# A four-layer transformer step on one core: queries moved ahead, layer norm and routing of the last batch in smaller steps, expert gathers six ahead

## The chip, the cores and the metric

The kernel runs on 1 core of a Trainium2 chip. The metric is device microseconds of one launch; the median of three runs is given. The engines in what follows: TensorE (PE) multiplies matrices, VectorE (DVE) and ScalarE (ACT) work on tiles of 128 rows, GpSimd (POOL) does the same more slowly and issues the indirect DMAs, SyncE (SP) issues most plain DMAs.

## What is computed

Four batches of 512 rows of 256 numbers, all in float32. Four layers, each added to x:

```
x = x + xattn0(layernorm(x), ctx)     # 1 head, 1601 context rows
x = x + ffn0(layernorm(x))            # 8 heads, 8 experts a head, hard gate, causal attention
x = x + xattn1(layernorm(x), ctx)     # 16 heads, masked, output projection
x = x + moe(layernorm(x))             # 32 experts, the best 8 a row, capacity 256

def moe(x):                           # x: 2048 x 256
    probs = softmax(x @ gate.T)       # 2048 x 32
    topw, topi = top_k(probs, 8);  topw /= topw.sum(-1)
    flat_e = topi.reshape(-1)
    pos = place of each choice in its expert's list, in order of the rows
    buf[flat_e, pos] = x[row]         # 32 x 256 x 256; places from 256 on are dropped
    h = silu(buf @ gate_half.T) * (buf @ up_half.T)      # 192 wide
    eo = h @ down.T
    return sum over the 8 choices of topw * eo[flat_e, pos]
```

## The kernel before

The 2048 rows of x are 16 tiles of 128 rows (NT = 16), four to a batch (TB = 4), and stay on the chip through all layers. A scheduler orders the first attention and the routing's own instructions by the order in the program; the second attention and the experts are ordered by hand, as generators whose steps are run between bursts of TensorE work: a `yield` is a place where the other stream gets its turn.

*First attention* (lines 180 to 312). `fold_weights` multiplies the query and key weights into one (TensorE `pw`, `pb`). `queries(b)` takes a batch's layer norm, transposes it (`tp_xn`, line 153), multiplies it by the folded weight (`pq`, line 225) and by the folded bias (`pc`, line 237). The loop over 16 tiles then makes scores (`sc`, line 255), their maximum on VectorE, the exponentials `pr` on ScalarE (line 267), and, one tile behind, transposes of the probabilities (`tp`, line 394), the sum over context rows (`po`, line 403) and, two tiles behind, the projection (`tp_o`, line 415; `pf`, line 421). The queries of batch b + 1 are made in two pieces, at tiles 2 and 3 of batch b. The loads stand on SyncE's queue: x of batch 0, weights, context of batch 0 transposed and by rows, value weight, then x of the other batches.

*Second attention* (lines 1178 to 1472). A burst of TensorE work makes scores for one stretch of keys (`sa`, line 1171, for the maxima `mx` on VectorE, line 1174; `sb`, line 1458, for the exponentials on ScalarE, line 1463, into probability tiles `pt`) and the sums `pv` (line 1391). Between bursts, steps of the next batch's projection and of the last batch's routing run. `finish(b)` (line 1355) closes a batch: it projects (`pf`, line 1372), adds to x (line 1375), two tiles a step, then hands over to `route_steps`.

*Layer norm*. `variances` (line 117) takes statistics of the four tiles (lines 122 and 123). `moments` takes the root by ScalarE's Sqrt (line 131) and a reciprocal; `moments_root` (line 95) takes it by a starting guess and three rounds of Newton's rule on small tiles (lines 101 to 113), on GpSimd, or on VectorE for the last batch.

*Routing* (`route_steps`, line 1647). For a batch: layer norm, transposes (line 1665), logits (1673), softmax, top-8 of each row (1700, 1701), a running count that gives each choice its place, weights (1737). Then for each tile one-hots: `r_lb` (VectorE, line 1742) of the place modulo 8, `r_hold` of it times the row's number (ScalarE, 1748) and times its weight (GpSimd, 1749), `r_ha` of the place over 8 (VectorE, 1753). 32 small products (`ph`, line 1761) put numbers and weights at their places; line 1766 adds them to `held`. Each of `r_lb`, `r_hold` and `r_ha` has one buffer. `slots` (line 1771) spreads `held` out into lists of rows (`ids`) and weights. Routing of batches 0 to 2 runs between bursts of the next batch's attention; that of the last batch has nothing beside it.

*Experts* (`experts1`, line 1475). For each of 32 experts: load weights (four ahead), gather its 256 rows by two indirect DMAs on GpSimd (line 1498), AHEAD = 8 experts ahead, transpose (line 1508), up-projection (`gu`, `gr`, line 1521), down-projection (`po_e`, line 1537), scaling on ScalarE (`eo`, line 1543), and an addition to the output rows by two indirect DMAs on GpSimd (line 1549). Additions of one expert wait until those of the expert before have landed, as they can add to the same rows. GpSimd issues gathers and additions in program order. The order at the heart:

```python
                for e in range(E1):
                    if e + 4 < E1:
                        load(e + 4)
                    if e + AHEAD < E1:
                        gather(e + AHEAD)
                    if e + 1 < E1:
                        transpose(e + 1)
                    up(e)
                    if e:
                        down(e - 1)
```

Of the kernel before, what the change touches and what calls it, by code (L numbers as in the profile page):

```python
# [12 lines left out]
F32 = mybir.dt.float32  # L13
# [3 lines left out]
ALU = mybir.AluOpType  # L17
# [4 lines left out]
P = 128  # L22
B, S, D = 4, 512, 256
S2 = 1601
NT = B * S // P
TB = S // P
# [13 lines left out]
Q1 = 401  # L40
LO = 8
HI = CAP // LO
AHEAD = 8
NO_SLOT = 4096.0

NEG = -3.0e38
# [6 lines left out]
class Program:  # L53
# [38 lines left out]

        return self.normed(b, pool, *self.moments(b, pool))

    def moments_root(self, b, pool, eng):


        nc = self.nc
        mv = self.variances(b, pool)
        v = pool.tile([P, TB], F32, name="ln_v")  # L100
        nc.vector.tensor_scalar(v, mv[:, :, 1], EPS, None, ALU.add)
        i = pool.tile([P, TB], I32, name="ln_i")
        nc.vector.tensor_scalar(i, v.bitcast(I32), 1, None, ALU.arith_shift_right)
        nc.vector.tensor_scalar(i, i, -1.0, float(0x5F3759DF), ALU.mult, ALU.add)
        h = pool.tile([P, TB], F32, name="ln_h")
        nc.vector.tensor_scalar(h, v, -0.5, None, ALU.mult)  # L106
        rstd = pool.tile([P, TB], F32, name="ln_rstd")
        y, a = i.bitcast(F32), v
        for _ in range(4):
            eng.tensor_tensor(a, y, y, ALU.mult)  # L110
            eng.tensor_tensor(a, a, h, ALU.mult)
            eng.tensor_scalar(a, a, 1.5, None, ALU.add)
            eng.tensor_tensor(rstd, a, y, ALU.mult)
            y = rstd
        return mv, y

    def variances(self, b, pool):
        nc = self.nc
        mv = pool.tile([P, TB, 2], F32, name="ln_mv")
        for t in range(TB):  # L120
            st = pool.tile([P, 6], F32, name="ln_st")
            nc.vector.bn_stats(st, self.xs[b * TB + t])
            nc.vector.bn_aggr(mv[:, t, :], st)
        return mv

    def moments(self, b, pool):

        nc = self.nc
        mv = self.variances(b, pool)
        rstd = pool.tile([P, TB], F32, name="ln_rstd")  # L130
        nc.scalar.activation(rstd, mv[:, :, 1], AF.Sqrt, bias=self.eps)
        return mv, rstd
# [54 lines left out]
    def xattn0(self, ve, oe, outer, dram):  # L187
# [3 lines left out]
        with ExitStack() as es:  # L191
# [13 lines left out]
            bk = self.load_column(wp, "L0_bk")  # L205
            ctxT, ctx, q = {}, {}, {}
            ctxT[0] = self.load_chunks(0, big)
            ctx[0] = self.load_rows(0, rows)
            wv = self.load_split(wp2, "L0_Wv", D)
            bv = self.load_row(wp2, "L0_bv")  # L210
            self.load_x(range(TB, NT))
            wg = self.f0_wg = self.load_split(outer, "F0_wg", H0 * E0)
            self.f0_xnT, self.f0_gate = {}, {}
            wqk, qb = self.fold_weights(wq, wk, bq, wp, ps_m)
            self.mask_scan(self.cp, scan, dram)

            def queries(b):

                xnT = self.transposed(self.layernorm(b, p1), p1, ps_m, "mm")
# [23 lines left out]
                q[b] = qT, kb  # L243
                yield

            for _ in queries(0):
                pass
            pending, late = None, None
            for i in range(NT):
                b, t = divmod(i, TB)  # L250
# [35 lines left out]
                            self.d[w][:, :P].rearrange("(k p) f -> p k f", p=P),  # L286
                        )
                project = self.xattn0_project(*late, wv, p2, ps_m) if late is not None else None
                if t == TB - 1 and b + 1 < B:
                    next(queried)  # L290
                late = None
                if pending is not None:
                    late = self.xattn0_sum(
                        *pending, ctx[(i - 1) // TB], bv, p2, ps_m, ps_o, project
                    )
                if t == TB - 2 and b + 1 < B:
                    queried = queries(b + 1)
                    next(queried)
                if t == 0 and b:
# [878 lines left out]
    def xattn1_keys(self, router):  # L1178
# [9 lines left out]
        with ExitStack() as es:  # L1188
# [41 lines left out]
            def project(b):  # L1230

                ctxT = ctx[b] = self.load_context(b, p1)
                mv, rstd = self.moments_root(b, p1, nc.gpsimd)
                yield True
                xn = self.normed(b, p1, mv, rstd, root=False)
                add_bias(b)
# [117 lines left out]

            def finish(b):

                for t0 in range(0, TB, 2):
                    oTs = []
                    for t in (t0, t0 + 1):
# [8 lines left out]
                    for t, oT in zip((t0, t0 + 1), oTs):  # L1368
                        x = self.xs[b * TB + t]
                        pf = ps_s.tile([P, D], F32, tag="s", name="pf")  # L1370
                        for k in range(2):
                            nc.tensor.matmul(  # L1372
                                pf, oT[:, k, :], fo[:, k, :], start=(k == 0), stop=(k == 1)
                            )
                        nc.vector.tensor_tensor(x, pf, x, ALU.add)
                    yield
                yield from router.route_steps(b, p1, ps_s, "s", ps_s, "s")

            def run(steps):
                for _ in steps:  # L1380
# [94 lines left out]
    def experts1(self, router):  # L1475
# [3 lines left out]
        with ExitStack() as es:  # L1479
# [85 lines left out]
            with tc.manual_schedule():  # L1565
# [5 lines left out]
                for e in range(E1):  # L1571
                    if e + 4 < E1:
                        load(e + 4)
                    if e + AHEAD < E1:
                        gather(e + AHEAD)
                    if e + 1 < E1:
                        transpose(e + 1)
                    up(e)
                    if e:
                        down(e - 1)  # L1580
                down(E1 - 1)

# [1 line left out]
class Router:  # L1584
# [59 lines left out]
        for _ in self.route_steps(b, p1, ps1, "s", pst, "t"):  # L1644
            pass

    def route_steps(self, b, p1, ps1, tag1, pst, tagt):

        nc, prog = self.nc, self.prog
        sh = [P, TB, E1]  # L1650
        last = b == B - 1
        mv, rstd = prog.moments_root(b, p1, nc.vector if last else nc.gpsimd)
        yield True
        xn = prog.normed(b, p1, mv, rstd, root=False)
        for t in range(b * TB, (b + 1) * TB):
            nc.sync.dma_start(prog.out[t * P : (t + 1) * P, :], prog.xs[t])
        nc.sync.dma_start(
# [38 lines left out]

        top = p1.tile([P, TB, TOPK], F32, name="r_top")
        rest = p1.tile(sh, F32, name="r_rest")
        for t in range(TB):
            nc.vector.max(top[:, t, :], pr[:, t, :])  # L1700
            nc.vector.match_replace(rest[:, t, :], top[:, t, :], pr[:, t, :], -1.0)
# [34 lines left out]
        nc.vector.reciprocal(den, den)  # L1736
        nc.vector.tensor_tensor(pr, pr, wide(den), ALU.mult)
        yield
        for t in range(TB):
            ll = [P, E1, LO]  # L1740
            lb = p1.tile(ll, F32, name="r_lb")
            nc.vector.tensor_tensor(  # L1742
                lb, lo[:, t, :].unsqueeze(2).to_broadcast(ll),
                self.count[:, :LO].unsqueeze(1).to_broadcast(ll), ALU.is_equal,
            )
            hold = p1.tile([P, E1, 2, LO], F32, name="r_hold")
            i = b * TB + t
            nc.scalar.activation(hold[:, :, 0, :], lb, AF.Copy, scale=self.tok1[:, i : i + 1])
            nc.gpsimd.tensor_tensor(  # L1749
                hold[:, :, 1, :], lb, pr[:, t, :].unsqueeze(2).to_broadcast(ll), ALU.mult  # L1750
            )
            ha = p1.tile([P, E1, HI], F32, name="r_ha")
            nc.vector.tensor_tensor(
                ha, hi[:, t, :].unsqueeze(2).to_broadcast([P, E1, HI]),
                self.count.unsqueeze(1).to_broadcast([P, E1, HI]), ALU.is_equal,
            )
            yield True
            ph = ps1.tile([P, E1 // 4, 2 * LO], F32, tag=tag1, name="ph")
            for g in range(E1 // 4):
                for s in range(4):  # L1760
                    nc.tensor.matmul(
                        ph[32 * s : 32 * s + 32, g, :], ha[:, 4 * g + s, :],
                        hold[:, 4 * g + s].rearrange("p v l -> p (v l)"), start=True, stop=True,
                        tile_position=(0, 32 * s),
                    )
            nc.vector.tensor_tensor(self.held, ph, self.held, ALU.add)
            yield
        if b == B - 1:
            self.slots(p1, ps1, tag1)

    def slots(self, p1, ps1, tag1):

# [115 lines left out]
```

## Time and profile before

| | us |
|---|---|
| three runs | 2241.95, 2233.48, 2243.65 |
| their median | 2241.95 |
| the profiled execution | 2232.17, its span 2230.3 |
| granted TensorE clock, mean of the span | 0.966 |
| last batch's routing, last `pf` to first gather | 1936.7 to 1981.35 |
| experts, first gather to the end | 1981.35 to 2230.3 |

In the profile's lines, times are microseconds from the start of the span. A line of the timeline has the start, the duration, the engine, the line of the kernel, the operation, output<-inputs, the shapes, and in brackets the idle time of the engine before it with what ended it. `PEclk` gives the clock that TensorE was granted in each of 40 slices, in tenths.

### The profile page before, as it was taken

How to read it: one execution, taken by the hardware profiler on the slowest of the kernel's cores; microseconds unless marked ns; L12 is line 12 of the kernel's file. 1: busy time of each engine (PE TensorE's matmuls, PEld its weight loads, DVE VectorE, ACT ScalarE, POOL GpSimd, SP SyncE). 2: the span in 40 equal slices, each digit the busy share in tenths (PEclk: the TensorE clock that was granted, in tenths of full speed). 3: DMA queues.
4: the chain of work that ended last, by engine and by line, in shares of the span. 5: the costliest groups of instructions: out<-in, count | busy, mean ns of one | idle time of the engine just before them, and what ended most of it. 6: DMA issues, size and time to landing. Idle time of an engine off the chain costs nothing.

```text
span 2230.3 us, 29813 instructions
## 1 busy us (share of the span) xinstructions
PE 2063.4 (93%) x11446; PEld 1066.8 (48%) x11446; DVE 1191.7 (53%) x1953; ACT 715.3 (32%) x1523; POOL 806.9 (36%) x865
## 2 busy tenths in 40 slices
PE   6999999999999999988999999999999999859893
PEld 4667754444444544334444444444444444347561
DVE  5344345445555444565657757785678775232220
ACT  1222221112122121103545545554455555412121
POOL 9999444545444444422100100010001000047764
PEclk9999999999999999999999999999999999969986
DMA  6473121122122223224221222123121200037763
GB/s 211 134 254 104 52 70 56 50 57 57 41 61 74 63 68 62 52 54 100 60 47 29 67 57 38 38 59 66 21 49 31 45 16 2 19 118 178 168 142 38
DMA packets 98190, 161.89 MB, mean 73 GB/s; under 512 B 20100, under 2 KB 68760, under 8 KB 97528
## 3 DMA queue, kind: packets, MB, share of 16 engines
q1 hardware_dynamic: 79800, 126.00, 22.2%
q0 software_dynamic: 17664, 33.38, 7.4%
q8 instruction: 93, 1.52, 0.3%
q14 instruction: 57, 0.47, 0.1%
q10 hardware_dynamic: 576, 0.52, 0.1%
HBM read 137.28 MB, written 22.31 MB: 72 GB/s over the span
## 4 chain that ended last, share of the span: by engine, by line
PE 50%; DVE 7%; DMA 4%; issue 2%; POOL 1%; ACT 1%; POOLq 0%; SPq 0%; ACTq 0%; DVEq 0%
PE sb L1458 12%; PE sa L1171 10%; PE pv L1391 8%; DVE mx L1174 4%; DMA out<-eo,ids 3%; PE acc L589 3%; PE py L885 2%; PE pv L1281 2%; PE po_e L1537 2%; PE pk L1253 2%; PE gu L1521 2%; POOL out L1549 1%; PE pf L1372 1%; DMA qd<-kc 1%; PE gr L1521 1%
## 5 line engine op out<-in xcount | busy, mean ns | idle before, releaser
L1174 DVE TENSOR_REDUCE mx<-sa 128x2 f32<-128x802 f32 x512 | 495.1, 990 | 139.1 <-PE sb L1458 72.4
L1463 ACT ACTIVATE pt<-sb 128x512 f32<-128x512 f32 (+1 forms) x832 | 429.6, 604 | 309.9 <-PE sb L1458 287.4
L1171 PE MATMUL sa<-kq,qq 32*128 32x401 f32 x2048 | 467.6, 542 | 35.6 <-DVE mx L1174 29.1
L1171 PEld LDWEIGHTS sa<-kq,qq 32*128 32x128 f32 x2048 | 172.3, 186 | 205.5 <-DVE mx L1174 170.9
L589 PE MATMUL acc<-og,oe 128*128 128x512 f32 x512 | 239.7, 597 | 2.4 <-DVE og L570 2.4
L885 PE MATMUL py<-ve,xnT 128*128 128x512 f32 x512 | 231.7, 595 | 3.3 <-DVE mx L1174 3.2
L1458 PE MATMUL sb<-b 32*128 32x512 f32 (+1 forms) x832 | 229.5, 637 | 0.0
L1458 PE MATMUL sb<-qs,ks 32*128 32x512 f32 (+1 forms) x832 | 224.4, 632 | 1.4 <-ACT pt L1463 1.1
L1391 PE MATMUL pv<-pt,v 128*32 128x512 f32 (+1 forms) x1664 | 197.0, 599 | 0.0
L890 DVE TENSOR_TENSOR y<-py,gm 128x1024 f32<-128x1024 f32 x64 | 78.4, 1224 | 209.1 <-PE py L885 152.4
L110 POOL TENSOR_TENSOR ln_v<-ln_i 128x4 f32<-128x4 f32 x6 | 1.2, 201 | 518.8 <-DVE ln_h L106 518.8
L527 POOL TENSOR_SCALAR pr<-pr,den 128x128 f32<-128x128 f32 (+3 forms) x128 | 144.0, 1136 | 123.8 <-DVE den L525 123.8
L899 POOL TENSOR_TENSOR y_a<-y 128x512 f32<-128x512 f32 x64 | 81.5, 1274 | 247.3 <-DVE y L890 100.1
L516 ACT ACTIVATE pr<-sc,nm 128x128 f32<-128x128 f32 (+3 forms) x128 | 66.4, 523 | 280.6 <-DVE nm L512 178.4
L1749 POOL TENSOR_TENSOR r_hold<-r_lb,r_pr 128x256 f32<-128x256 f32 x16 | 23.7, 1479 | 358.5 <-DVE r_lb L1742 284.3
L885 PEld LDWEIGHTS py<-ve,xnT 128*128 128x128 f32 x512 | 95.5, 190 | 118.0 <-issue 112.4
L589 PEld LDWEIGHTS acc<-og,oe 128*128 128x128 f32 x512 | 91.1, 190 | 90.3 <-issue 85.3
L1458 PEld LDWEIGHTS sb<-qs,ks 32*128 32x128 f32 (+1 forms) x832 | 87.3, 180 | 79.5 <-issue 34.9
L1458 PEld LDWEIGHTS sb<-b 32*128 32x128 f32 (+1 forms) x832 | 87.7, 184 | 76.9 <-issue 33.4
L1549 POOL DMA_INDIRECT out<-eo,ids x64 | 101.8, 1590 | 57.2 <-ACT eo L1543 38.4
L1399 DVE TENSOR_TENSOR ov<-pv,ov 128x512 f32<-128x512 f32 x64 | 44.2, 690 | 133.5 <-PE pv L1391 133.5
L570 DVE TENSOR_TENSOR og<-gb,oT 128x512 f32<-128x512 f32 x128 | 114.7, 936 | 0.5
(277 smaller groups left out, 2763.2 us busy)
## 6 DMA issues: line engine op xcount, KB each, us to landing
gb<-gd SPq DMA_DIRECT2D x128, 256.0 KB
mi<-in_mask POOLq DMA_DIRECT2D x32, 401.0 KB, 3.9
wgu<-in_E_gu SPq DMA_DIRECT2D x32, 384.0 KB
qq<-qd SPq DMA_DIRECT2D x64, 128.0 KB
kq<-kd SPq DMA_DIRECT2D x64, 100.2 KB
ctxT<-in_ctxT SPq DMA_DIRECT2D x8, 800.5 KB
ctxT<-in_ctxT SPq DMA_DIRECT2D x12, 512.0 KB
ctx<-in_ctx SPq DMA_DIRECT2D x12, 512.0 KB
```

The lines of the kernel that those rows point to most:

```text
L527: nc.gpsimd.tensor_scalar(pr[:, j, :n], pr[:, j, :n], den[:, j : j + 1], None, ALU.mult)
L570: nc.vector.tensor_tensor(og, gb[:, i, :], oT[s], ALU.mult)
L589: nc.tensor.matmul(acc[b][m], oe[hp][:, c : c + P], og, start=(hp == 0 and e == 0), stop=(hp == NP - 1 and e == E0 - 1),)
L885: nc.tensor.matmul(py[:, j, :], xnT[:, k, t * P : (t + 1) * P], ve[:, k, j, :], start=(k == 0), stop=(k == 1),)
L890: nc.vector.tensor_tensor(y, py.rearrange("p j (e k) -> p (j e) k", e=E0), gm[:, t, hp * 16 : hp * 16 + 16].unsqueeze(2).to_broadcast([P, ...
L899: nc.gpsimd.tensor_tensor(a, yy[:, :, :h4], yy[:, :, h4:], ALU.add)
L1171: nc.tensor.matmul(pa[:, j, :Q1], qq[r, s, t * P : (t + 1) * P], kq[r, s, :], start=True, stop=True)
L1174: nc.vector.tensor_reduce(mx[:, t, s, 2 * half : 2 * half + 2], pa[:, :, :Q1], AX.X, ALU.max)
L1391: nc.tensor.matmul(pv[32 * s : 32 * s + 32, :], v1[b % 2][:r, kt, h * VW : h * VW + 32], pts[s][:r, :], start=(kt == held[0][0]), stop=(kt ...
L1458: nc.tensor.matmul(sb[:r, :], ks[i % 2][q, kt * P : kt * P + r], qs[i % 2][q, :], start=True, stop=True,)
L1463: nc.scalar.activation(pt[:r, :], sb[:r, :], AF.Exp)
L1549: i = nc.gpsimd.indirect_dma_start(out=view, out_offset=bass.IndirectOffsetOnAxis(ap=router.ids[:, e, c : c + 1], axis=0), in_=eo[:, c, :] ...
```

## The change

1. *First attention.* x of batch 1 is loaded before the context rows of batch 0. The transposes of batch 0 come before the folding of the weights. The queries of batch 1 are made in one go, between the scores of tile 0 and tile 1; those of batches 2 and 3 stay at tiles 2 and 3 of the batch before.
2. *Routing of every batch* has one more `yield`, ahead of the top-8; the one-hot `r_ha` is made in two halves of 16 experts.
3. *Routing of the last batch.* `finish` takes the statistics of each tile right behind its addition (`variance`), the root is ScalarE's Sqrt (`moments`) in place of Newton's rule on VectorE. The one-hots go into buffers of the pool of probability tiles `pt`, so that those of several tiles exist at a time, and the products of a tile (now `hold`) are issued behind the one-hots of the next.
4. *Experts.* AHEAD is 6 and the pool of gathered rows 16 buffers (was 20). The transposes of expert 1 come after the up-projection of expert 0, and the down-projection and addition of expert 0 right behind them.

```diff
-AHEAD = 8
+AHEAD = 6
...
-    def moments(self, b, pool):
+    def variance(self, b, t, mv, pool):
+        st = pool.tile([P, 6], F32, name="ln_st")
+        self.nc.vector.bn_stats(st, self.xs[b * TB + t])
+        self.nc.vector.bn_aggr(mv[:, t, :], st)
+
+    def moments(self, b, pool, mv=None):
         nc = self.nc
-        mv = self.variances(b, pool)
+        if mv is None:
+            mv = self.variances(b, pool)
         rstd = pool.tile([P, TB], F32, name="ln_rstd")
         nc.scalar.activation(rstd, mv[:, :, 1], AF.Sqrt, bias=self.eps)
         return mv, rstd
...
             ctxT[0] = self.load_chunks(0, big)
+            self.load_x(range(TB, 2 * TB))
             ctx[0] = self.load_rows(0, rows)
...
-            self.load_x(range(TB, NT))
+            self.load_x(range(2 * TB, NT))
...
-            wqk, qb = self.fold_weights(wq, wk, bq, wp, ps_m)
-            self.mask_scan(self.cp, scan, dram)
...
-            for _ in queries(0):
-                pass
+            queried = queries(0)
+            next(queried)
+            wqk, qb = self.fold_weights(wq, wk, bq, wp, ps_m)
+            self.mask_scan(self.cp, scan, dram)
+            next(queried)
...
-                if t == TB - 1 and b + 1 < B:
+                if i == 0:
+                    for _ in queries(1):
+                        pass
+                if t == TB - 1 and 0 < b < B - 1:
                     next(queried)
...
-                if t == TB - 2 and b + 1 < B:
+                if t == TB - 2 and 0 < b < B - 1:
                     queried = queries(b + 1)
                     next(queried)
...
             def finish(b):
+                mv = p1.tile([P, TB, 2], F32, name="ln_mv") if b == B - 1 else None
...
                         nc.vector.tensor_tensor(x, pf, x, ALU.add)
+                        if mv is not None:
+                            self.variance(b, t, mv, p1)
                     yield
-                yield from router.route_steps(b, p1, ps_s, "s", ps_s, "s")
+                free = ptp if b == B - 1 else None
+                yield from router.route_steps(b, p1, ps_s, "s", ps_s, "s", mv, free)
...
-                    if e + 1 < E1:
+                    if 0 < e < E1 - 1:
                         transpose(e + 1)
                     up(e)
-                    if e:
+                    if e == 0:
+                        transpose(1)
+                        down(0)
+                    elif e > 1:
                         down(e - 1)
...
-        mv, rstd = prog.moments_root(b, p1, nc.vector if last else nc.gpsimd)
-        yield True
-        xn = prog.normed(b, p1, mv, rstd, root=False)
+        if last:
+            xn = prog.normed(b, p1, *prog.moments(b, p1, mv))
+        else:
+            mv, rstd = prog.moments_root(b, p1)
+            yield True
+            xn = prog.normed(b, p1, mv, rstd, root=False)
...
         rest = p1.tile(sh, F32, name="r_rest")
+        yield True
         for t in range(TB):
             nc.vector.max(top[:, t, :], pr[:, t, :])
...
         for t in range(TB):
-            ll = [P, E1, LO]
-            lb = p1.tile(ll, F32, name="r_lb")
+            if free is not None:
+                lb = free.tile([P, S], F32, name="pt")[:, : E1 * LO]
+                hold = free.tile([P, S], F32, name="pt")
+                has = [free.tile([P, S], F32, name="pt") for _ in range(2)]
+            else:
...
-            nc.vector.tensor_tensor(
-                ha, hi[:, t, :].unsqueeze(2).to_broadcast([P, E1, HI]),
-                self.count.unsqueeze(1).to_broadcast([P, E1, HI]), ALU.is_equal,
-            )
+            hh = [P, E1 // 2, HI]
+            for j, ha in enumerate(has):
+                e = slice(E1 // 2 * j, E1 // 2 * (j + 1))
+                nc.vector.tensor_tensor(
+                    ha, hi[:, t, e].unsqueeze(2).to_broadcast(hh),
+                    self.count.unsqueeze(1).to_broadcast(hh), ALU.is_equal,
+                )
+            if free is not None and t == 0:
+                self.behind = has, hold
+                continue
+            if free is not None:
+                (has, hold), self.behind = self.behind, (has, hold)
             yield True
...
+            self.hold(has, hold, ps1, tag1)
+            yield
+        if free is not None:
+            self.hold(*self.behind, ps1, tag1)
             yield
```

`hold` is the body of the old loop from `ph` on: the 32 products and the addition to `held`.

## The prediction

> **What bounds the kernel now.** I read the shares of busy time, the slices and the chain of waits first.
>
> ```profile
> PE 2063.4 (93%) x11446; PEld 1066.8 (48%) x11446; DVE 1191.7 (53%) x1953; ACT 715.3 (32%) x1523; POOL 806.9 (36%) x865
> PEclk9999999999999999999999999999999999969986
> ...
> PE 50%; DVE 7%; DMA 4%; issue 2%; POOL 1%; ACT 1%; POOLq 0%; SPq 0%; ACTq 0%; DVEq 0%
> ```
>
> TensorE is busy for 93% of the span, at full clock except in the slices from about 1900 us on. So time saved in the long middle must be TensorE work or TensorE idling; the last 290 us are another matter. I then read, by time, the four places that the change touches.
>
> Start of the first attention, TensorE alone:
>
> ```profile
> 38.27 8.20 PE L255 MATMUL sc<-ctxT,qT 128*128 128x512 f32 x16 [5.43 <-ACT pr L267]
> ...
> 60.87 0.39 PE L415 MATMUL tp_o<-ident,o 128*128 128x128 f32 x2
> ...
> 75.42 3.65 PE L225 MATMUL pq<-xnT,wqk 128*128 128x512 f32 x8
> 78.90 1.84 PE L237 MATMUL pc<-fold_k,xnT 128*128 128x1 f32 x16
> 80.61 0.41 PE L415 MATMUL tp_o<-ident,o 128*128 128x128 f32 x2
> ...
> 83.70 1.75 PE L255 MATMUL sc<-ctxT,qT 128*128 128x512 f32 x2 [1.26 <-ACT pr L267]
> ...
> 98.06 0.39 PE L415 MATMUL tp_o<-ident,o 128*128 128x128 f32 x2
> ```
>
> There is a hole of 5.43 us before the second tile's scores, which then take 8.20 (later ones take 5.71). The second batch's queries sit among the cycles from 60.87 to 98.06.
>
> Batch 0's top-8 (VectorE from 1428.35 to 1433.2), as TensorE feels it:
>
> ```profile
> 1434.17 0.94 PE L1171 MATMUL sa<-kq,qq 32*128 32x401 f32 x4 [2.35 <-DVE mx L1174]
> ```
>
> Last batch, layer norm and then the first one-hot round, all engines:
>
> ```profile
> 1936.78 0.42 DVE L1375 TENSOR_TENSOR x<-pf,x 128x256 f32<-128x256 f32 x1 [0.44 <-PE pf L1372]
> ...
> 1943.69 1.38 DVE L140 TENSOR_SCALAR ln_xn<-x,ln_mv,ln_rstd 128x256 f32<-128x256 f32 x4
> ...
> 1944.24 2.21 PE L1665 MATMUL tp_xn<-ident,ln_xn 128*128 128x128 f32 x8 [7.50 <-DVE ln_xn L140]
> ```
> ```profile
> 1958.10 0.42 DVE L1742 TENSOR_TENSOR r_lb<-r_lo,count 128x256 f32<-128x256 f32 x1
> ...
> 1958.69 1.45 POOL L1749 TENSOR_TENSOR r_hold<-r_lb,r_pr 128x256 f32<-128x256 f32 x1 [92.33 <-DVE r_lb L1742]
> ...
> 1960.20 1.06 PE L1761 MATMUL ph<-r_hold,r_ha 128*32 128x16 f32 x64 [4.28 <-POOL r_hold L1749]
> 1961.32 0.29 DVE L1766 TENSOR_TENSOR held<-ph,held 128x128 f32<-128x128 f32 x1 [1.67 <-PE ph L1761]
> 1961.53 0.41 DVE L1742 TENSOR_TENSOR r_lb<-r_lo,count 128x256 f32<-128x256 f32 x1
> ```
>
> Here every engine stands in one chain: tile 2's first one-hot starts when tile 1 has gone all the way round, 3.43 us later.
>
> Experts, GpSimd alone:
>
> ```profile
> 1981.35 1.12 POOL L1498 DMA_INDIRECT xg<-normed,ids  x1 [10.95 <-issue]
> ...
> 2006.60 1.67 POOL L1549 DMA_INDIRECT out<-eo,ids  x1 [0.30 <-issue]
> ...
> 2014.39 1.62 POOL L1549 DMA_INDIRECT out<-eo,ids  x1 [1.63 <-ACT eo L1543]
> ...
> 2219.43 1.55 POOL L1549 DMA_INDIRECT out<-eo,ids  x1 [3.07 <-DMA out<-eo,ids]
> ```
>
> 20 gathers precede the first addition; the additions then run in a chain, each waiting for its forerunner to land. From 2006.60 to 2219.43 there are 31 intervals of 6.865 us, while TensorE needs 5.49 an expert (up-projections' starts 1996.90 and 2002.39). The end is the first addition plus that chain.
>
> **Part by part.** All against the profiled run: 2232.17 us, span 2230.3.
>
> *Early first queries.* Undisturbed cycles, tp_o to tp_o, take 13.67 (98.06, 111.73, 125.40). The two that hold the queries take 80.61 − 60.87 = 19.74 and 98.06 − 80.61 = 17.45, so queries cost 19.74 + 17.45 − 2 × 13.67 = 9.85. Their matmuls are 1.04 + 3.65 + 1.84 = 6.53; the rest is stalls. Moved into the hole of 5.43 before the second scores, and warming the clock for these (8.20 − 5.71 = 2.49), the hole takes up most: 5.43 + 2.49 = 7.92, at most. What is given back: TensorE now transposes batch 0 before it folds the weights. The fold, at 10.29 today, waits for the transposes (1.94), which wait for layer norm (about 15); queries then end 0 to 3 us later, today 24.16. The additional layer norm on VectorE in the same stretch, its rows up to 4.51 long there against 1.38, can delay the second maxima by about 1. On SP four loads of x pass ahead of four context row loads; the values are needed only at 49.44 (first po), so I cost them at nothing, and where that cover goes, the first po is late. 7.92 less half of 3 and a part of that 1: I take 6, bounds −3 (the full delay, nothing hidden) and 7.9.
>
> *Choices in two steps*, batches 0 to 2. VectorE's excursion of 4.85 keeps the maxima that TensorE waits for. A yield splits off its first 1.2 us (sum, reciprocal, scale, from 1428.35 to 1429.53); a stall of 2.35 can fall by this at most. Batch 0 and batch 1 (1673.96) both show 2.35. At 0.8 each of three batches: 2.4 (0 to 3.6). The one-hots in halves of 512 cost two starts rather than one and lie under scores.
>
> *Statistics by tiles, root by ScalarE.* From the last addition's end to the first ln_xn there are now four pairs of statistics (0.43 and 0.18, from 1937.12 to 1939.79) and 20 small VectorE operations (1939.83 to 1943.65). Three pairs go between the additions, which wait for TensorE anyway (0.44 and 1.44 idle). Left behind the last: one pair, 0.65; Sqrt, 0.30 as at 7.49 (line 131); reciprocal, 0.18 as at 1428.66. First ln_xn 1937.37 + 0.65 + 0.34 + 0.25 = 1938.6 (the last two with their starts) rather than 1943.69: 5.1. A table load (1.28 at 1951.52) has ScalarE's idle time, which begins at 1934.97, for cover; uncovered, the gain is 3.8.
>
> The clock: granted 1.00 from 1937 to 1940, 0.61 from 1940 to 1944, 0.50 after. It fell some 4 us after the last matmul of 1936.74. The gap before the transposes shrinks from 7.50 to about 2.4, so these eight may take 1.04 as at 69.00 and not 2.21, with a little for the logits: 1.5 (0 to 2).
>
> [...]
>
> *One-hots in probability tiles, products a tile behind.* Four rounds today, lb 0.42, GpSimd's hold 1.45 to 1.48, products 1.06, sum 0.29: from 1958.10 to the next stage at 1971.92, 13.82. With separate buffers VectorE writes lb and both ha without waiting, so GpSimd's four holds (1.45 + 0.05) follow one another, paced by VectorE's 1.6 to 1.75 a tile: hold 4 ends about 7.25 after the start, products 1.06 and sum 0.35 behind it, and the next stage's wait 0.05: 8.8. Saved 5.0 (4 to 5.5). A yield finds no other work in this batch.
>
> *Experts.* Each expert has two gathers; look-ahead 6 and not 8 leaves 14 ahead of the first addition. At 1.253 apart (2005.34 − 1981.35 over 19 gathers is 1.263, over the last 18 1.253) the 14th starts at 1982.77 + 12 × 1.253 = 1997.8 and the addition at 1999.05, if its expert's output is there: the first up-projection starts at 1992.25 today behind the second expert's transposes, for which a gather had to land; after, it follows its own, landed by 1990, through 4.3 of up-projection, 0.7 of transposes, 2.5 of down-projection and a copy: about 1998.6. So 7.5 earlier. But four gathers now lie between first and second addition, not two: 1.67 + 0.3 + 1.57 + 0.3 + 4 × 1.33 = 9.1 or so, where 7.79 was taken: 6.3 left. Intervals with gathers mean 7.03, those without 6.48, and two more have gathers where nothing else waits; 6.0 to 6.3. I take 6.0 (3 to 7). Nothing is queued behind a late gather but additions, and each gather is issued some six intervals ahead of its use.
>
> Sum: 6 + 2.4 + 5.1 + 1.5 + 5.0 + 6.0 = 26.0; 2232.2 − 26 = 2206 for a run like the profiled one. The median shown, 2241.95, is 9.8 above that run, so for a median 2216.
>
> **Rivals.** *The start gives nothing* (the fold behind layer norm costs what the hole takes up). For it: the fold waits for nothing but its weights today, and TensorE has no other work from 10.29 on. Against: the hole of 5.43 is there to be filled. 20 us gained: 2222; with the worst bound of −3, 2225.
>
> *The first addition stays late*, since outputs, not gathers, set it. For it: 1998.6 and 1999.05 are close, and cold TensorE (0.50 until about 1995) stretches the up-projection (3.52 against 1.89). Then some 4 of 6 are lost: 2220.
>
> *Slower: the addition chain stretches.* More gathers fall among additions while weights and gathers load the DMA (share 0.94 from 1980 to 1995, 0.65 to 2010); the first intervals of 7.8, 7.8 and 8.0 there are the longest. It outweighs the rest where the mean of the 31 intervals passes 6.865 + 26/31 = 7.7. If all went at 7.8, 31 × 0.935 = 29 are lost: 2245. Against: from the fourth interval on 6.5 to 7.0 hold with gathers in them, and the number of gathers is unchanged.
>
> *It does not do what it says*: holds or copies wait for probability tiles still read, or a ScalarE table load falls into the chain. The router's part (5.1 + 1.5 + 5.0) would fall to some 5: 2222.
>
> **How the numbers follow.** Forecast 0.55; start nothing 0.17; addition late 0.11; router half 0.10; slower side 0.07. The shown runs spread by 10, so 0.5%, 11 us, is about what a measurement of this kernel tells from no change: faster means under 2230.7. Over the parts' bounds the gain is 8 (all lowest) to 31 (all highest). A new median may also stand by the profiled run, 9.8 lower, so the low end is 2241.95 − 31 − 9 = 2202; the high end, 2230, leaves out the corner in which several parts fail at once, and most of the slower side. Within 0.5% are the tails of the three middle rivals, two failing together (0.07), and the half of the slower side that is not beyond 2253 (0.04): 0.11. Slower 0.03, left of that side. Faster 0.86.
>
> **What would show it.** Right: the second batch's queries on TensorE between the first two score groups and a cycle of 13.7 after 61; a first ln_xn within 2 us of the last addition; four holds on GpSimd about 1.7 apart; 14 gathers and a first addition 17 to 18 us behind the first gather, then 31 intervals near 6.9. Wrong: a hole of over 5 still ahead of the second scores; intervals above 7.2; a clock of 0.50 in the transposes (1.5 of the sum).

## The result, and the profile after

The changed kernel takes 2211.01 us (median of 4 runs, 2208.91 to 2213.27), the kernel before 2239.57 on the same chip (4 runs, 2233.48 to 2243.65): a ratio of 0.9878, 95% interval 0.9854 to 0.9902. That is 28.6 us by the medians, where 26 was forecast (and a median of 2216). The profiled execution is the slowest of the four, 2213.27, span 2211.5, so the two profiles differ by only 18.8. In a repeat (e1, below) the span was 2202.2. The table cuts the spans at places that all three have.

| stretch, us | before | after | after, repeat (e1) |
|---|---|---|---|
| start to the last `tp_o` of the first attention | 289.90 | 274.72 | 276.28 |
| from there to the last `pf` of the second attention | 1646.46 | 1653.06 | 1646.53 |
| from there to the first gather (last batch's routing) | 44.99 | 35.16 | 35.14 |
| first gather to the last expert's addition | 238.08 | 237.78 | 233.43 |
| from there to the end | 10.91 | 10.82 | 10.85 |
| sum | 2230.34 | 2211.54 | 2202.23 |

The first lines of the page of the changed kernel, the clock by slices, and the engines' shares of the chain that ended last:

```profile
PE 2065.1 (93%) x11446; PEld 1065.5 (48%) x11446; DVE 1189.0 (54%) x1950; ACT 720.6 (33%) x1526; POOL 798.1 (36%) x865
...
PEclk9999999999999999999999999999999999859996
...
PE 50%; DVE 7%; DMA 3%; issue 3%; POOL 2%; ACT 0%; SPq 0%; another core or an unknown queue 0%; ACTq 0%; POOLq 0%; DVEq 0%
```

TensorE's work is the same; what is shorter is the time in which it idles. The start, TensorE alone:

```profile
13.35 2.40 PE L156 MATMUL tp_xn<-ident,ln_xn 128*128 128x128 f32 x8 [13.35 <-DVE ln_xn L143]
...
18.81 3.68 PE L226 MATMUL pq<-xnT,wqk 128*128 128x512 f32 x8
...
23.58 1.96 PE L259 MATMUL sc<-ctxT,qT 128*128 128x512 f32 x4
...
33.67 3.70 PE L226 MATMUL pq<-xnT,wqk 128*128 128x512 f32 x8 [1.64 <-DVE xnT L159]
...
38.91 5.79 PE L259 MATMUL sc<-ctxT,qT 128*128 128x512 f32 x16
...
57.42 0.39 PE L422 MATMUL tp_o<-ident,o 128*128 128x128 f32 x2
...
71.09 0.39 PE L422 MATMUL tp_o<-ident,o 128*128 128x128 f32 x2
```

The queries of batch 1 fill the hole ahead of the second scores; these run at the full clock (1.00, and 5.79 for 16 of them; 8.20 at a mean of 0.71 before), and the next cycles take 13.67. The first scores come earlier (23.58, before 25.26), although the folding now waits for layer norm.

The last batch's layer norm, all engines:

```profile
1928.36 0.39 DVE L1383 TENSOR_TENSOR x<-pf,x 128x256 f32<-128x256 f32 x1
...
1930.00 1.38 DVE L143 TENSOR_SCALAR ln_xn<-x,ln_mv,ln_rstd 128x256 f32<-128x256 f32 x4
...
1930.56 1.83 PE L1683 MATMUL tp_xn<-ident,ln_xn 128*128 128x128 f32 x8 [2.40 <-DVE ln_xn L143]
```

TensorE's gap is 2.40 and not 7.50. Then the one-hots of the first tile and the beginning of the second:

```profile
1944.04 0.42 DVE L1772 TENSOR_TENSOR pt<-r_lo,count 128x256 f32<-128x256 f32 x1
1944.38 1.72 DVE L1784 TENSOR_TENSOR pt<-r_hi,count 128x512 f32<-128x512 f32 x2
...
1944.68 0.87 POOL L1778 TENSOR_TENSOR pt<-pt,r_pr 128x256 f32<-128x256 f32 x1 [80.10 <-DVE pt L1772]
...
1945.60 1.18 PE L1809 MATMUL ph<-pt 128*32 128x16 f32 x64 [3.74 <-POOL pt L1778]
1946.02 0.41 DVE L1772 TENSOR_TENSOR pt<-r_lo,count 128x256 f32<-128x256 f32 x1
```

The second tile's first one-hot no longer waits for the first tile's products. GpSimd's hold takes 0.87 where it took 1.45, and the two halves 1.72 where the whole took 1.22: the same inputs, another division of the time. More of that below. GpSimd in the experts:

```profile
1979.38 0.95 POOL L1509 DMA_INDIRECT xg<-normed,ids  x1 [0.30 <-issue]
1984.08 1.66 POOL L1560 DMA_INDIRECT out<-eo,ids  x1 [3.75 <-ACT eo L1554]
...
1993.26 1.62 POOL L1560 DMA_INDIRECT out<-eo,ids  x1 [0.53 <-issue]
```

The last of the 14 gathers is done, and GpSimd waits 3.75 for the first output. What held it, all engines:

```profile
1976.01 0.73 PE L1519 MATMUL tp_e<-ident,xg 128*128 128x128 f32 x4
...
1976.58 2.52 PE L1548 MATMUL po_e<-wdn,hT 128*128 128x256 f32 x8
...
1981.84 0.69 DVE L1523 COPY xT<-tp_e 128x512 f32<-128x512 f32 x1 [4.75 <-remote]
...
1983.32 0.84 ACT L1554 ACTIVATE eo<-po_e,share 128x256 f32<-128x256 f32 x2 [6.69 <-remote]
```

"remote" is a releaser that the profile can't name. By their semaphores both instructions wait for TensorE, and TensorE's matmuls for them should have ended, by these rows, at 1976.74 and 1979.10: 5.1 and 4.2 us before VectorE and ScalarE begin. The trace has TensorE's own signals at 1981.82 and 1983.30, so it is these that came late. In the profile before, the same two followed within 0.1.

### The profile page after: what moved, and what is told of

The parts are those of the page before. It is cut to its first block, busy times and chain, and to the rows that moved or that the text cites. A ratio compares the mean times of both kernels' runs of the same rounds, so it can differ in the third digit from the quotient of the medians.

```text
span 2211.5 us, 29816 instructions
## 1 busy us (share of the span) xinstructions
PE 2065.1 (93%) x11446; PEld 1065.5 (48%) x11446; DVE 1189.0 (54%) x1950; ACT 720.6 (33%) x1526; POOL 798.1 (36%) x865
## 4 chain that ended last, share of the span: by engine, by line
PE 50%; DVE 7%; DMA 3%; issue 3%; POOL 2%; ACT 0%; SPq 0%; another core or an unknown queue 0%; ACTq 0%; POOLq 0%; DVEq 0%
PE sb L1469 12%; PE sa L1178 11%; PE pv L1402 8%; DVE mx L1181 4%; PE acc L596 3%; DMA out<-eo,ids 3%; PE py L892 3%; PE pv L1288 2%; PE pk L1260 2%; PE po_e L1548 1%; POOL out L1560 1%; PE gu L1532 1%; PE pf L1380 1%; POOL xg L1509 1%; PE po L562 1%
## 5 line engine op out<-in xcount | busy, mean ns | idle before, releaser
L1778 POOL TENSOR_TENSOR r_hold<-r_lb,r_pr 128x256 f32<-128x256 f32 x12 | 11.4, 946 | 285.8 <-DVE r_lb L1772 269.5
```

## Experiments

Ratios are to the kernel before, measured on the same chip together with the kernel in question (its median was 2229.46 beside e1 to e4, 2230.95 beside e5 to e8 and 2235.21 beside e9 to e12). Kernels are the changed one with the edit shown, where nothing else is said.

**e1, the changed kernel again.** No edit.

> The changed kernel once more, unaltered. Its first profile had the first addition 21.1 us behind the first gather (17.7 forecast), because expert 1's copy on VectorE and expert 0's scaling on ScalarE began 4 to 5 us after TensorE's matmuls for them. If that delay belongs to the kernel, it stands here again: 21 us, and the delays 4 to 5. If it was a mishap of that execution: first addition 17.5 to 18.5 behind the first gather and delays under 0.5. The granted clock fell to 0.5 for 6.8 us from 1901 in that profile; if that was chance too, the span here is 3 to 4 us shorter, and the last projection ends by 1925. Time 2206 to 2213.

2205.18 us, ratio 0.9893 (0.9874 to 0.9913). GpSimd in the experts:

```profile
1974.39 0.94 POOL L1509 DMA_INDIRECT xg<-normed,ids  x1 [0.30 <-issue]
1975.63 1.66 POOL L1560 DMA_INDIRECT out<-eo,ids  x1 [0.30 <-issue]
...
1984.58 1.62 POOL L1560 DMA_INDIRECT out<-eo,ids  x1 [0.30 <-issue]
```

The first addition stands right behind the last gather, 17.69 behind the first gather (1957.95), and neither copy nor scaling is late by more than 0.3. The half clock from 1901 is gone too, and the second stretch of the table is 6.5 shorter. So the wait of the first profile does not belong to every execution. The runs of the other kernels show that it is no single mishap either (end of this section).

**e2, experts as before:** `AHEAD = 8`, transposes of e + 1 ahead of every up-projection, `down(e - 1)` behind it.

```diff
-AHEAD = 6
+AHEAD = 8
...
-                    if 0 < e < E1 - 1:
+                    if e + 1 < E1:
                         transpose(e + 1)
                     up(e)
-                    if e == 0:
-                        transpose(1)
-                        down(0)
-                    elif e > 1:
+                    if e:
                         down(e - 1)
```

> The changed kernel with the experts' order and look-ahead of before (8, transposes of expert 1 first). The prediction's theory: 6 us slower than the changed kernel, 2217. Rival, from the two profiles (first gather to last addition 238.08 before, 237.78 after): the expert part is worth 0 to 1, time as the changed kernel, 2210 to 2212. First gather to first addition 25.3, intervals' mean 6.87.

**e3, look-ahead 8, new order:** the first of the two hunks alone.

> The changed kernel with look-ahead 8, its new order kept: 18 gathers ahead of the first addition and not 14. If gathers set the first addition: 18 x 1.253 + 0.2 = 22.7 behind the first gather. If the delay on VectorE and ScalarE comes with the new order, it shows here too, at the same place, but lies under the gathers, and the first addition is 22.7 all the same. First interval 9 (two gathers each: 7.8, since only two lie between). Time within 3 of the changed kernel.

**e4, look-ahead 6, old order:** the second hunk alone.

> The changed kernel with look-ahead 6 but expert 1's transposes ahead of the first up-projection and the first down-projection behind the second up-projection. Gathers allow the first addition 17.5 to 18 behind the first gather; the old order had the first output 21 to 21.5 behind it (2002.0 + 0.4 against 1981.35), so 21 to 21.5. If this equals the changed kernel's 21.1, the new order brings nothing beside its delay; if the changed kernel shows 17.7 in the repeat, the order is worth 3.5. Time 0 to 4 above the changed kernel.

| | us | ratio (95%) | first gather to first addition | then to the last | together |
|---|---|---|---|---|---|
| e1, 6 and new order | 2205.18 | 0.9893 (0.9874 to 0.9913) | 17.69 | 215.74 | 233.43 |
| e2, 8 and old order | 2210.99 | 0.9915 (0.9898 to 0.9931) | 25.26 | 213.61 | 238.87 |
| e3, 8 and new order | 2209.42 | 0.9910 (0.9893 to 0.9926) | 22.69 | 213.89 | 236.58 |
| e4, 6 and old order | 2209.83 | 0.9907 (0.9890 to 0.9927) | 22.74 | 212.91 | 235.65 |

The expert part is worth 5.8 by the medians of e1 and e2, as forecast, though the intervals of the ratios overlap, and 5.4 by these two profiles. By the profiles the look-ahead gives 3.2 and the order 2.2, whichever is done first. That split is not settled: by the medians the look-ahead alone gives 1.2 and the order alone 1.6, and e8 (below), whose expert code is that of e1, takes 235.62 for this stretch (17.71 and 217.92), 2.2 more than e1. Each by itself brings the first addition 2.5 earlier, both together 7.6; but 1.9 to 2.8 of that (4.3 in e8) are paid back in the additions behind when both are done. e3's first addition came at 22.69, where 22.7 was expected; e4's first addition was 1.2 to 1.7 later than expected, since its up-projection started later behind the gathers and ran at half the clock (its 8 `gu` took 3.62, those of the next expert 1.89).

**e5, part 1 alone** on the kernel before.

> The kernel before with part 1 alone (x of batch 1 loaded early, transposes ahead of the folding, queries of batch 1 behind the first scores). The prediction's term: 6 us faster, bounds -3 to 7.9. Rival, from the first two profiles (last tp_o of the first attention at 289.90 and 274.72): 15 us faster, of which 13.3 by the fourth tp_o and the rest at the queries of batch 2; 1 to 2 of it may be lost again in the layer behind.

2221.09, ratio 0.9957 (0.9945 to 0.9969): 9.9 us by the medians, between the term's 6 and the rival's 15. The last `tp_o` stands at 278.34, 11.6 earlier. In the profiled execution 5 of these are lost later, in stretches where this code is that of before and the clock falls to 0.50 for 3.4 or 6.8 us at a time (41 us at half the clock in the second stretch of the table, 24 before).

**e6, only the queries moved**, on the kernel before: the two hunks with `if i == 0` and `0 < b`, without loads and folding.

> The kernel before with only the queries of batch 1 moved between the first two score groups; loads and folding stay. They then need x of batch 1, whose loads stand behind the context rows and the value weight on SyncE. If the loads are early enough: first score group as before (25.26), hole filled, last tp_o some 12 us earlier. If x comes too late, TensorE waits for it ahead of the second scores, and 3 to 6 us of gain are left. The prediction costed this load at nothing and did not say what the kernel gets without it.

2232.19, ratio 0.9998 (0.9979 to 1.0016). Four runs took 2224 to 2225 and six 2231 to 2237; the profiled one is of the four. TensorE in it:

```profile
22.21 1.96 PE L255 MATMUL sc<-ctxT,qT 128*128 128x512 f32 x4
...
35.22 2.07 PE L255 MATMUL sc<-ctxT,qT 128*128 128x512 f32 x2 [5.43 <-ACT pr L267]
37.49 0.47 PE L153 MATMUL tp_xn<-ident,ln_xn 128*128 128x128 f32 x1 [0.20 <-DVE ln_xn L140]
```

The hole of 5.43 stands, as before: layer norm of batch 1 is not done when it opens, and score matmuls come first, with the queries in the midst of them. x of batch 1 is issued on SyncE from 16.21 here and from 9.07 in e5, its statistics on VectorE begin at 26.88 and not at 17.69, and its root on ScalarE, 23.32 in e5, stands at 36.48, behind the first tile's exponentials and a table load (1.28 in the profiles before and after). e6 leaves out the early loads and the late folding together, so these times point to the loads, but no run separates the two. Without them the move does not fill the hole; it only spares the later cycles their stalls. The last `tp_o` stands at 281.70, 8.2 earlier than before. Of that, 3.05 lie ahead of the first scores, where the code is that of before: here the clock was full from 15.25 and the eight `pq` took 3.70, in the profile before it was full from 22.62 and they took 5.80. What the six slower runs lose besides was not profiled and stays open.

**e7, loads and folding alone**, on the kernel before; the queries stay among the tiles.

> The kernel before with only the loads of batch 1's x early and the transposes ahead of the folding; the queries of batch 1 stay among the tiles. The prediction charged 0 to 3 us for the fold's wait for layer norm. Rival, from the changed kernel's profile (first scores at 23.58 and not 25.26): the fold runs at the full clock behind the transposes and pq takes 3.68 and not 5.80, so first scores are 1.5 to 2 us EARLIER; but the hole ahead of the second scores stays, so the time as a whole is within 2 us of before.

2231.68, ratio 1.0005 (0.9995 to 1.0015). First scores at 24.52, the second at

```profile
37.54 8.00 PE L256 MATMUL sc<-ctxT,qT 128*128 128x512 f32 x16 [5.44 <-ACT pr L268]
```

The first scores come 0.7 earlier and not 1.5 to 2, the hole and its slow scores remain (8.00 for 16, where 5.79 is taken at the full clock), and there is no time in it. So e6 and e7 bring nothing in the median that can be told from no change, and together, as e5, 9.9.

**e8, choices in one step:**

```diff
         rest = p1.tile(sh, F32, name="r_rest")
-        yield True
         for t in range(TB):
```

> The changed kernel without the added yield ahead of the top-8. The prediction: 2.4 us slower; TensorE's wait at the top-8 is 2.35 again in batches 0 and 1, where the changed kernel has 0.88. Rival: the added step moves all later ones by a burst, and in batch 0 the last one-hot product then waits 2.00 for GpSimd, with the clock at 0.5 for 6.8 us behind it; without the yield this wait is gone, and the time is equal or 1 to 2 us shorter. From the profile the step of before had neither, so I expect the stretch from batch 0's closing projection to batch 1's 240 to 241 and not 243, and the time within 2 us of the changed kernel.

2206.50, ratio 0.9900 (0.9880 to 0.9919), where e1 had 0.9893: no difference. TensorE at the top-8 of batch 0 in e8:

```profile
1418.87 0.94 PE L1178 MATMUL sa<-kq,qq 32*128 32x401 f32 x4 [2.35 <-DVE mx L1181]
```

And in e1, at the same place and at the last tile's products of that batch:

```profile
1426.04 0.60 PE L1178 MATMUL sa<-kq,qq 32*128 32x401 f32 x2 [0.88 <-DVE mx L1181]
...
1472.16 0.99 PE L1809 MATMUL ph<-r_hold,r_ha 128*32 128x16 f32 x64 [2.00 <-POOL r_hold L1778]
```

The step takes 1.47 from one wait and puts 2.00 elsewhere: everything behind it comes a burst later, and the fourth tile's products are then asked for before GpSimd has its half. From the start of one closing projection to the next, batches 0 to 3 take 240.14 + 142.50 + 177.86 = 560.50 in e8 and 243.09 + 140.12 + 177.62 = 560.83 in e1: behind batch 0 the step loses 3.0, and behind batch 1, where the products do not wait, it gains 2.4.

**e9, TensorE kept busy.** Matmuls into a tile that nobody reads, added to the last batch's routing:

```diff
+    def fill(self, n, ps1, tag1):
+        at = ps1.tile([P, D], F32, tag=tag1, name="fill")
+        for _ in range(n):
+            self.nc.tensor.matmul(at, self.prog.ident, self.prog.xs[0], start=True, stop=True)
```

> The changed kernel with 43 matmuls of 128x256 added in the last batch's routing, into a PSUM tile that nobody reads, only to keep TensorE busy in its gaps: 4 ahead of the transposes, 8 behind the logits, 8 behind the running count, 2 behind each of three rounds of products, 13 behind the spread of the lists. If idle time is what takes the clock down (0.50 from 1927 to 1971 in the repeat of the changed kernel): clock at 1.00 for most of the stretch, transposes 1.04 and not 1.74, 16 logit matmuls 1.9 and not 3.8, spread of the lists (pd, 7.02) 3.5 to 4.5, last projection to first gather 28 to 30 and not 35.14; time 5 to 7 less, 2198 to 2200 where the changed kernel has 2205. Rival: the clock stays at 0.50; the added matmuls then take 0.76 each and delay the count by 1.6 and the first products by 2.3, time 2 to 4 more.

2206.38, ratio 0.9864 (0.9835 to 0.9894). Two windows of e1 (routing of the last batch), and below them two of e9; the last three columns are granted clock, DMA share and GB/s:

```profile
1927.00:1948.00 21.00, 9.27 (x277) 7.88 (x274) 15.98 (x51) 3.83 (x7) 3.62 (x4) 0.50 0.08 27
1948.00:1958.00 10.00, 7.12 (x136) 6.91 (x128) 1.53 (x9) 0.00 (x0) 0.05 (x1) 0.50 0.02 3
```
```profile
1932.00:1951.50 19.50, 17.85 (x319) 13.96 (x318) 15.98 (x52) 3.84 (x7) 3.63 (x4) 0.91 0.08 29
1951.50:1957.90 6.40, 5.95 (x133) 5.48 (x134) 1.37 (x9) 0.00 (x0) 0.04 (x1) 0.82 0.07 7
```

The clock was held, and the spread of the lists (`pd`) took

```profile
1951.69 3.76 PE L1839 MATMUL pd<-held,spread 32*128 32x16 f32 x128 [0.42 <-DVE held L1827]
```

where e1 had 7.02. Last projection to first gather: 30.21, not 35.14. So in this stretch it is idle time that takes the clock down: 0.50 with the gaps, 0.91 and 0.82 with them filled. The time as a whole does not show the 5 to 7 that were expected: in this execution the first addition came 21.01 behind the first gather with TensorE's outputs late by 3.4 and more, and the additions took 218.41. Against the changed kernel (0.9893 and 0.9878) the gain is not settled.

**e10, look-ahead 5; e11, the wide one-hot in four operations of 256; e12, e9 and e10 together.**

> The changed kernel with look-ahead 5: 12 gathers ahead of the first addition. Gathers would allow it 15.2 behind the first gather, but the first output is there at 16.6 (in the repeat of the changed kernel, scaling from 1974.12 with the first gather at 1957.95), so 16.6 to 16.8; two more gathers fall among the additions, at 0.46 each (from 8 to 6, four gathers moved cost 1.85 there): intervals' sum 216.7. Net 0, time as the changed kernel within 2. If instead the additions had slack for gathers, 1 us less.

> The changed kernel with the wide one-hot made in four operations of 256 and not two of 512. Theory: GpSimd's hold needs about 0.48 and otherwise waits for the VectorE operation in progress to end, and the next VectorE operation waits for it; before, 1.48 = 0.98 left of an operation of 1.22, + 0.48; now 0.92 = 0.43 left of 0.68, + 0.48. Then here 0.6 to 0.7, and one quarter takes 0.34 + 0.48 = 0.8. Each tile's one-hots take longer by two starts, about 0.15. Rival: the hold became faster for another reason (its buffers), and stays at 0.92. Time within 2 of the changed kernel.

> The additions of the busy TensorE and look-ahead 5 together. If the clock is held, the first output comes some 2.5 earlier (up-projection of 3.6 and 1.9 at half the clock), the first addition is then bound by its 12 gathers, 15.2 behind the first gather, and the time is 1 to 2 below the kernel with the busy TensorE alone. If the clock is not held, as look-ahead 5 alone.

e10: 2209.00, 0.9885 (0.9862 to 0.9907); first addition 18.07 behind the first gather, the rest 218.48. Nothing gained: the outputs do not come sooner. What the two gathers cost among the additions is not told from e8's 217.92. e12: 2209.04, 0.9878 (0.9855 to 0.9900), 18.14 and 219.67; the 15.2 that the gathers allowed was missed, since TensorE's outputs were late again. e11: 2211.98, 0.9886 (0.9861 to 0.9911). A tile of the last batch in it:

```profile
1949.65 1.85 DVE L1784 TENSOR_TENSOR pt<-r_hi,count 128x256 f32<-128x256 f32 x4
...
1949.90 0.65 POOL L1778 TENSOR_TENSOR pt<-pt,r_pr 128x256 f32<-128x256 f32 x1 [1.12 <-DVE pt L1772]
```

The hold now takes 0.65, and one of the quarters 0.85 where the other three take 0.41: as the theory of turns said. (In the first tile the hold took 0.94: two quarters went ahead of it.)

**TensorE's late outputs.** How much later than the modelled end of its matmuls the first scaling (`eo` of expert 0) began, and the first addition behind the first gather: first profile 4.2 and 21.14, e1 0.0 and 17.69, e8 0.0 and 17.71, e9 3.4 and 21.01, e10 1.0 and 18.07, e11 3.6 and 20.53, e12 0.1 and 18.14. Expert 1's copy was late by 2.7 in e10 and by 4.2 in e12. In the profiles with look-ahead 8 or the old order (before, e2 to e7) neither was late by over 0.5. Why is open. A full DMA does not tell the two groups apart: its share in the ten microseconds ahead is 0.98 and 1.08 in the first profile (1965 to 1975), and 0.95 and 1.08 in e1 (1960 to 1970).

What does go with the delay is a loss in the traces themselves. In the five executions with late outputs most records of landed DMA parts are missing from the first gather on: 68 to 148 are left in its first 20 us, where the other nine executions have 461 to 512. Ahead of the first gather none is missing in any of them (11402 to 11404 each). Whether the delay and the loss have one cause, or the recording itself holds TensorE's signals up, no run tells, and what TensorE waited for can't be read there. So a first addition in one of these five profiles is weak evidence on the kernel.

## Why the prediction held, step by step

**The sum** was 26.0; the profiles give 18.8 and 28.1, the medians 28.6 and 24.3. The sum is right, several of its terms are not, and that their errors cancel is luck.

**Early first queries, 6 forecast: 15.2 and 13.6 in the stretch, 9.9 in the time when alone.** The mechanism was right, its size was not. The step that failed is "7.92, at most": the hole's size and the slow clock behind it (0.71 over the second scores) were taken as the limit of the gain, with the 9.85 that the queries cost among the tiles beside it. But those 9.85 are saved wherever the queries go, and the hole only decides what they cost there. By the rows: from the end of the first scores to the second, 31.16 to 38.91, is 7.75, where 32.83 to 38.27 was 5.44, so they cost 2.3, and the second scores are 8.20 − 5.79 = 2.4 shorter. With 1.50 of waiting for a copy gone, 9.85 − 2.3 + 2.4 + 1.5 = 11.4. From the first scores to the fourth `tp_o` it is 111.73 − 25.26 = 86.47 before and 98.44 − 23.58 = 74.86 after: 11.6 (e1 74.58, e5 74.57).

The delay of 0 to 3 at the fold did not show: in these two profiles the first scores are 1.7 earlier. But that is no gain of the edit that the runs could show. It hangs on when TensorE's clock rises, which differs from execution to execution (full from 22.62 before, from 15.25 in e6, from 17.01 in the first profile of the changed kernel): with the new start the first scores begin at 23.4 to 25.9 in twelve profiles, with the old one at 25.26 and, in e6, at 22.21. The rival "the start gives nothing" falls, though either half of the edit comes near it: e7 gives nothing, and e6 6 to 7 us in four runs of ten and nothing in six. That the early loads cost nothing was right; that the gain hangs on them (or on the folding, which e6 leaves out too) was not said.

**Choices in two steps, 2.4 forecast: 0.** The wait was cut as said (2.35 to 0.88, twice). What failed is costing the step by that wait alone: it shifts all later steps of the routing by a burst, and these have waits of their own (e8). Behind batch 1 the gain came (2.4), behind batch 0 a loss of 3.0 took it back.

**Statistics and root, 5.1 forecast: 5.1.** Last projection to first normalised row 7.32 before, 2.22 after. The table load (1.28) was hidden, at 1926.41.

**The clock, 1.5 forecast: 0.4.** First normalised row to the maximum of the logits took 6.78 and takes 6.41. The granted clock still fell, some 3.8 us after the last projection had ended (0.50 from 1931.9, in e1 from 1927.0), over the transposes, with a gap of 2.40 ahead of them and not 7.50. The step that failed is that the shorter gap would leave the eight transposes at the full clock: they took 1.83, where 1.04 was forecast and 2.21 was taken before. What such transposes do to the clock the runs do not settle: it fell over these, and at the start of the same profile eight of them (from 13.35) and then 1.5 us of the fold were all of TensorE's work ahead of 17.01, where the trace has the clock full. With the gaps filled (e9) the clock held over the same transposes, and the 16 logit matmuls behind them took 2.16 and not 3.82. The transposes still took 1.64, as they follow the normalised rows, but the maximum of the logits stood 4.93 behind the first of these rows, 1.5 less than 6.41.

**One-hots, 5.0 forecast: 4.35.** 13.82 became 9.46. The order was right. The term that was mis-sized is VectorE's pace, 1.6 to 1.75 a tile in the prediction and 2.17 in the trace: the second half of each one-hot takes 1.11 and not 0.68, since it waits for GpSimd's hold. The hold itself took 0.87 to 0.92 and not 1.45.

**Experts, 6.0 forecast: 0.3, 4.65 (e1) and 2.5 (e8) by the profiles, 5.8 by the medians of e1 and e2.** 17.7 for the first addition was right in e1, and the longer first interval too (8.95, forecast 9.1). The intervals' sum grew by 2.1 (e1 against e2) to 5.1 (e8 against before) and not by 1.5: the intervals behind the first, costed at 0.3 at most, took the rest. The rival "the first addition stays late" did come about in the first profile, by a wait that the prediction did not know and that the runs do not explain.

**The slower side**, intervals of 7.7 and more: the mean was 6.99 and 6.96. **It does not do what it says** did not come about either: the holds wait for nothing but their one-hots and VectorE's turns, and the routing as a whole fell by 9.8 (44.99 to 35.16), where 11.6 was forecast.

## What to carry to other kernels

Work that leaves a crowded place saves what it cost there, stalls included; the hole it goes to decides only what it costs anew, and a hole is filled only if the operands are there when it opens (e5 against e6). A yield that shortens one wait moves every step behind it, so the later waits have to be read too. Two profiles of one kernel can differ by a third of what a change is worth: here 18.8 and 28.1 for the same edit. So a part of a few microseconds needs more than one profile of each kernel, and a stretch that no edit touched (the start in e6) shows how much is chance.

## What the runs showed of the hardware

**The hold on GpSimd and the one-hots on VectorE took turns by whole operations.** In the profile before, the VectorE operation beside the first hold (1.45 from 1958.69) is

```profile
1958.44 1.22 DVE L1753 TENSOR_TENSOR r_ha<-r_hi,count 128x1024 f32<-128x1024 f32 x1
```

The hold (two inputs, 128x256) begins beside a VectorE operation with two inputs and ends about 0.5 us after it, at each of the three lengths that were run: 1.45 beside 1.22, 0.87 beside 0.68, 0.65 beside 0.41. The next VectorE operation then takes 0.44 longer (1.12 for 0.68, 0.85 for 0.41). These times are what turns by whole operations give; what makes the two wait for each other no run shows. Shorter operations beside the hold shortened its wait, but both together took no less: from the start of the wide one-hot to the end of both it is 1.71 before, 1.72 with halves and 1.85 with quarters.

**The granted clock fell in steps of 3.41 us.** Of its 28 stretches at 0.50 in the profiles before and after, 24 last 3.41 or 6.83, two last 54.6 and 44.4, from the last batch's routing on, and two reach the end of the span. It fell also where TensorE has no gap (0.52 and 0.50 from 1901 to 1908 in the first profile, with none in the records from 1893 on). In the second stretch of the table the first profile has 41 us at half the clock and e1 20, and the stretch is 6.5 longer. Kept busy (e9), TensorE did the same spread of lists in 3.76 and not 7.02.
